# Transposed attention scores: one bank per head carried over four key tiles by key differences, and values kept by chunk

## The chip, the cores and the metric

One core of a Trainium2 chip runs the whole kernel. The metric is the device time of one execution in microseconds; before the change three runs gave a median of 2320.5 (2316.85 to 2321.68). The engines are named as in the profile: PE is TensorE's matmuls and PEld its weight loads, DVE is VectorE, ACT is ScalarE, POOL is GpSimd, SP is SyncE, which here only issues DMAs. Every engine works through its own instructions in order.

## The reference, cut to what matters

A transformer block with conditioning, for x of shape (2, 2048, 512), 16 heads of 32, hidden size 2048:

```
mod = silu(condition) @ Wada + bada            # shift, scale and gate, twice
xm  = layernorm(x) * (1 + sc_a) + sh_a
q, k, v = split(xm @ Wqkv)
attn = softmax(where(causal, q k^T / sqrt(32), -inf))
x   = x + gt_a * ((attn @ v) @ Wproj + bproj)
xm  = layernorm(x) * (1 + sc_m) + sh_m
x   = x + gt_m * (gelu(xm @ W1 + b1) @ W2 + b2)
```

## The kernel before, in words

The two batches (rows in the code) run one after the other: the QKV projection of 2048 tokens, the attention, the output projection. The MLP follows for both.

**QKV projection** (`Qkv.group`, L811). Four groups g of 512 tokens. In each, for the four chunks f of 128 channels (four heads), a tile of queries and a tile of keys is made in a PSUM bank, transposed (channels by tokens). ACT copies it in rounded form into `hl[:, 0]` (L830), DVE writes what the rounding left into `hl[:, 1]` (L831), and SP stores both to DRAM (L836). After chunk 0 the keys and queries are loaded again as `kst` and `qst` (L316, L325): for each head, the 128 partitions hold two parts of 32 channels, twice, in an order in which one matmul over 128 partitions yields the sum of all products of parts. Then come four tiles of values; ACT copies each into `vv` (L852), which holds all 2048 tokens by 512 channels of the batch. Between the projection's matmuls PE already computes scores of the first units, for their row maxima.

**Attention** (`attention_phase`, L541). A unit is a chunk c of four heads and a block i of 512 queries, 16 units per batch. For chunk 0 the blocks come in the order 0 to 3, then 0, 2, 1, 3. There are two kinds of scores. The first, tiles named `s`, have queries on partitions (`Row.bank`, L442): DVE takes their row maxima (L461, and L456 for masked ones). They are computed up to three units ahead, and `Row.score` (L494) puts them between other matmuls; the number for each step follows from `due` (L675), which spreads them over the steps by a weight for each. They use two PSUM banks. When a unit's maxima are complete, `split` (L464) divides each into three bf16 parts on DVE, and `rows` (L516) transposes them into `fold`.

The second kind, tiles named `st`, have keys on partitions (`scores_t`, L550). A step is one tile of 128 keys by 512 queries for four heads (unit i has 4i full steps, then three masked ones). Four matmuls put minus the maximum into the four heads' banks (`sel` times `fold`, 32 partitions, L575); then for each head one matmul adds the scores, and ACT writes the exponential into `e` (L593). The scores of the first kind stand between them, four or five per step as a rule: two in the two `s` banks, one in a bank borrowed from the four for `st` (L611), and again one in an `s` bank. Two steps later come the value matmuls `o` (L637). POOL adds the tiles of a group of four steps (L623), so that the row sums `sm` need one set of matmuls for four steps; in a batch's last unit DVE does this. POOL also masks (L602).

**Weights of the MLP.** During the projection POOL loads, combines and stores pieces of W1 and W2 (`Quarters`, L898), then combines W1 further (`FirstLayer`, L972), in rooms of the tag `w49`: two buffers of 7 x 512 values per partition.

Of the kernel before, what the change touches and what calls it, by code (L numbers as in the profile page):

```python
# [27 lines left out]
def dit_block_kernel(  # L28
# [69 lines left out]
    ones = bp.tile([P, P], F32, tag="ones", name="ones")  # L98
# [8 lines left out]
    nc.vector.tensor_scalar(sel, ones, -1.0, None, ALU.mult)  # L107
# [61 lines left out]
    ]  # L169
    n_early = (C - 1) * NQ  # L170
# [118 lines left out]
    class Row:  # L289


        def __init__(self, b):
            self.b = b
            self.vv = bp.tile([P, NT, D], F32, tag="vv", name="vv")
            self.kst, self.qst, self.pools = {}, {}, {0: bp}
            self.at = 0
            self.todo = [
                (u, h, t, kb)
                for u, (_, i) in enumerate(units)
                for h in range(HC)  # L300
                for t in range(TQ)
                for kb in range(i + 1)
            ]
            self.mx = None
            self.spent = 0
            self.rows_made = 0

        def load_keys(self, c, g, n=1):

            tok = slice(g * MT, (g + n) * MT)  # L310
            if g == 0:
                self.kst[c] = self.pools[c % 2].tile(
                    [P, HC, T], F32R, tag=f"kst{c % 2}", name="kst"
                )
            for r in range(4):
                nc.sync.dma_start(  # L316
                    self.kst[c][r * HD : (r + 1) * HD, :, tok].bitcast(F32),
                    kd[self.b][c][r % 2, :, tok].rearrange("(h d) t -> d h t", d=HD),
                )

# [220 lines left out]
    def attention_phase(row):  # L541
        b, vv, kst, qst = row.b, row.vv, row.kst, row.qst
        with pool(f"att{b}") as ap, pool(
# [4 lines left out]
            n_bank = [0]  # L548

            def scores_t(u, step, n):  # L550
# [21 lines left out]
                for h in range(HC):  # L572
                    g = slice(h * HD, (h + 1) * HD)
                    st = st_bank()
                    mm(  # L575
                        st[:, :w], sel[g, :], fold[u % 2][g, q0 : q0 + w],
                        start=True, stop=False,
                    )
                    sts.append(st)
                for h in range(HC):  # L580
                    at = 0
                    for j, q in tiles:
                        mm(
                            sts[h][:, at : at + QB - q],
                            kst[c][:, h, j * P : (j + 1) * P],
                            qst[u][:, h, q:],
                            start=False, stop=at + QB - q == w,
                        )
                        at += QB - q
# [94 lines left out]
            for u, (c, i) in enumerate(units):  # L684
                if NQ <= u + AHEAD < len(units):
                    row.load_queries(u + AHEAD)
                if u % NQ == 0 and c + 1 < C:
                    row.load_keys(c + 1, 0, NG)
                steps = len(steps_of[u])
                for n_step, tiles in enumerate(steps_of[u]):  # L690
                    last = n_step == steps - 1
# [37 lines left out]
                    def values(es=es, tiles=tiles, c=c, o=o, first=n_step == 0, last=last):  # L729
                        tile_by_tile(  # L730
                            o,
                            lambda j, h: vv[:, j, (c * HC + h) * HD : (c * HC + h + 1) * HD],
                            es, tiles, first, last,
                        )

                    def row_sums(es, last, tiles=((0, 0),), sm=sm, summed=summed):
                        first = not summed
                        summed.add(len(summed))
                        tile_by_tile(sm, lambda j, h: ones[:, :HD], es, tiles, first, last)
# [29 lines left out]
    class Qkv:  # L769
# [41 lines left out]
        def group(self, g, hp, between, among):  # L811
# [5 lines left out]
            n = 0  # L817
            for f in range(C):
                for which in range(2):
# [18 lines left out]
                    )  # L838
                    between(n)
                    n += 1  # L840
                if f == 0:
                    row.load_keys(0, g)
                    row.load_queries(g)
            for t in range(MTT):
# [7 lines left out]
                nc.scalar.copy(row.vv[:, g * MTT + t, :], ps)  # L852
# [41 lines left out]
    piece = 7 * C // 2 * P  # L894
# [77 lines left out]
    class FirstLayer:  # L972
# [8 lines left out]
        def load(self):  # L981
            if self.at < 7:
                room = self.pool.tile([P, 7, C * P], F32, tag="w49", name="w49", bufs=2)
                act(load_blocks(nc.gpsimd, room, 1, self.at))
# [3 lines left out]
        def step(self):  # L988
# [4 lines left out]
            n, room = self.rooms.pop(0)  # L993
            for k in range(4):
                room_sum(room, 1, k)
            act(nc.gpsimd.dma_start(w1e[n], room))
# [209 lines left out]
    with pool("qkv1") as qp, pool("ps_qkv1", bufs=6, space=PSUM) as ps_mm:  # L1206
# [18 lines left out]
        with pool("hl1") as hp:  # L1225
            late = FirstLayer(hp)

            def also(g, n):
# [3 lines left out]
                elif n % 2 == 0:  # L1232
                    late.step()

            def rooms():
                w = hp.tile([P, 7, C * P], F32, tag="w49", name="w7", bufs=2)
                w = w.rearrange("p n d -> p (n d)")
                return [w[:, k * piece : (k + 1) * piece] for k in range(2)]
# [3 lines left out]
            assert quarters.at >= FC and late.at == 7 and not late.rooms  # L1242
# [7 lines left out]
    HK = C // 2  # L1250
# [674 lines left out]
```

## Time and profile before

| | |
|---|---|
| median of three runs | 2320.5 us |
| the profiled execution | 2323.1 us |
| its span | 2321.4 us |
| granted TensorE clock | 0.998 |
| PE busy | 2270.8 us |
| DVE busy | 1582.5 us |
| POOL busy | 1290.9 us |
| first and last maximum matmul, batch 0 | 213.4 and 735 us |
| first and last maximum matmul, batch 1 | 997 and 1525 us |

Times in a row are microseconds from the span's start. A matmul's end is modelled, so matmuls that run into each other show lengths that overlap; the distance between two starts is the better price. What stands in brackets is the idle time of that engine before the instruction, and the instruction that ended it. A row "x4" is four instructions of one kind in a row.

### The profile page before, as it was taken

To read this page: it belongs to the slowest core of one execution; us is meant where nothing else is said; L and a number is where in the kernel's file an instruction comes from. 1 tells how busy PE (TensorE), PEld (TensorE's weight loads), DVE (VectorE), ACT (ScalarE), POOL (GpSimd) and SP (SyncE) were. 2 spreads that over 40 slices of the span, in tenths; PEclk is the share of its full clock that TensorE was granted. 3 is DMA by queue.
4 is the path that set the end of the run, shared out by engine and by line. 5 is a ranking of instruction groups with operands and counts; after the bars stand their busy time and mean duration, and the time that the engine had idled before them with its cause. 6 is when DMAs were issued, how large, how long until landed. Compare 5 with 4: busy or idle time off the path is not lost. (4 is left out here: it accounts for less than half of the span.)

```text
span 2321.4 us, 33398 instructions
## 1 busy us (share of the span) xinstructions
PE 2270.8 (98%) x12141; PEld 1388.8 (60%) x12141; DVE 1582.5 (68%) x3117; ACT 914.6 (39%) x1744; POOL 1290.9 (56%) x1036
## 2 busy tenths in 40 slices
PE   8999999999999999999999999999999999999998
PEld 4455545455544444555455554446888888888887
DVE  3366776777666735677667777555896876877787
ACT  2112555555565021155555554622332152251230
POOL 1052987878793663478788886653764602602510
PEclk9999999999999999999999999999999999999999
DMA  7577216151233799981522404265375554654643
GB/s 257 185 243 204 55 28 133 29 119 47 74 115 127 241 297 298 320 235 24 113 48 48 100 24 134 81 206 205 118 279 200 199 186 146 212 173 151 216 143 116
DMA packets 118524, 355.60 MB, mean 153 GB/s; under 512 B 14496, under 2 KB 15052, under 8 KB 103640
## 3 DMA queue, kind: packets, MB, share of 16 engines
q1 hardware_dynamic: 107040, 293.64, 41.9%
q0 software_dynamic: 10944, 59.28, 7.0%
q8 instruction: 96, 1.57, 0.3%
q14 instruction: 68, 0.56, 0.1%
q10 hardware_dynamic: 376, 0.55, 0.1%
HBM read 253.80 MB, written 107.48 MB: 156 GB/s over the span
## 5 line engine op out<-in xcount | busy, mean ns | idle before, releaser
L593 ACT ACTIVATE e<-st 128x512 f32<-128x512 f32 (+1 forms) x1152 | 573.1, 579 | 411.6 <-PE st L203 350.5
L461 DVE TENSOR_REDUCE mx<-s 128x1 f32<-128x512 f32 x604 | 408.0, 687 | 185.0 <-PE s L203 183.6
L623 POOL TENSOR_TENSOR ee<-ee,e 128x1024 f32<-128x1024 f32 x212 | 498.8, 2385 | 8.3 <-ACT e L593 8.3
L203 PE MATMUL s<-kst,qst 128*128 128x512 f32 (+3 forms) x1032 | 466.5, 453 | 15.9 <-DVE mx L461 6.3
L203 PE MATMUL st<-qst,kst 128*128 128x512 f32 (+3 forms) x1280 | 410.1, 387 | 0.0
L203 PE MATMUL ps_a<-sum,room 128*128 128x256 f32 x1504 | 357.4, 382 | 6.6 <-DVE c L1409 3.8
L203 PEld LDWEIGHTS ps_a<-sum,room 128*128 128x128 f32 x1504 | 281.5, 190 | 56.0 <-issue 8.7
L203 PE MATMUL o<-e,vv 128*32 128x512 f32 (+3 forms) x2560 | 300.8, 539 | 0.8 <-POOL e L602 0.8
L203 PEld LDWEIGHTS s<-kst,qst 128*128 128x128 f32 x1032 | 194.5, 189 | 174.0 <-DVE mx L461 58.6
L456 DVE CUSTOM_DVE_ANT_0 junk<-s,causal 128x512 bf16<-128x512 f32 (+3 forms) x428 | 209.2, 489 | 126.2 <-PE s L203 118.7
L203 PEld LDWEIGHTS st<-qst,kst 128*128 128x128 f32 x1280 | 227.5, 188 | 96.8 <-issue 66.7
L623 POOL TENSOR_TENSOR ee<-e 128x1024 f32<-128x1024 f32 x84 | 198.4, 2384 | 130.5 <-ACT e L593 130.4
L203 PE MATMUL ps_qk<-xmT,wqkv 128*128 128x512 f32 x512 | 240.5, 597 | 1.8 <-DVE xmT L263 1.8
L602 POOL TENSOR_SCALAR_AFFINE_SELECT e<-e 128x256 f32<-128x256 f32 x256 | 103.8, 436 | 107.2 <-ACT e L593 74.2
L203 PEld LDWEIGHTS ps_qk<-xmT,wqkv 128*128 128x128 f32 x512 | 94.2, 190 | 97.7 <-issue 91.4
L1637 POOL TENSOR_TENSOR c<-c,h 128x512 f32<-128x512 f32 x40 | 58.2, 1474 | 160.8 <-ACT c L1635 160.8
L203 PE MATMUL ps_b<-sum,room 128*128 128x256 f32 x608 | 143.6, 379 | 0.0
L203 PEld LDWEIGHTS ps_b<-sum,room 128*128 128x128 f32 x608 | 115.0, 190 | 15.4
L203 PE MATMUL ps_v<-wqkv,xmT 128*128 128x512 f32 x256 | 122.3, 594 | 0.0
L203 PEld LDWEIGHTS o<-e,vv 128*32 128x32 f32 x2560 | 60.8, 108 | 101.1 <-issue 83.4
L203 PE MATMUL st<-fold,sel 32*128 32x512 bf16 (+1 forms) x1152 | 116.1, 372 | 3.6 <-DVE mhl L482 2.6
L461 DVE TENSOR_REDUCE mx<-st 128x1 f32<-128x512 f32 x164 | 112.7, 687 | 4.9 <-PE st L203 2.7
(179 smaller groups left out, 2869.6 us busy)
## 6 DMA issues: line engine op xcount, KB each, us to landing
qst<-q SPq DMA_DIRECT2D x128, 256.0 KB
room<-w1e SPq DMA_DIRECT2D x28, 1024.0 KB
kst<-k SPq DMA_DIRECT2D x24, 1024.0 KB
room<-w1e SPq DMA_DIRECT2D x28, 768.0 KB
room<-w2e SPq DMA_DIRECT2D x21, 1024.0 KB
q<-hl SPq DMA_DIRECT2D x32, 512.0 KB
k<-hl SPq DMA_DIRECT2D x32, 512.0 KB
room<-w2e SPq DMA_DIRECT2D x21, 768.0 KB
```

The source lines that it names most:

```text
L203: return tc.keep_in_program_order(nc.tensor.matmul(*args, **kw))
L456: nc.vector.tensor_tensor_reduce(junk[:, :w], s[:, :w], causal[:, QB - w :], 1.0, MASKED, ALU.add, ALU.max, m,)
L461: nc.vector.tensor_reduce(m, s[:, :w], axis=AX.X, op=ALU.max)
L593: act(nc.scalar.activation(e[:, h % 2, :w], sts[h][:, :w], AF.Exp))
L602: nc.gpsimd.affine_select(d, d, pattern=[[0, 2], [1, P]], compare_op=ALU.is_ge, fill=0.0, base=0, channel_multiplier=-1,)
L623: act(engine.tensor_tensor(dst, x, y, ALU.add))
L1637: nc.gpsimd.tensor_tensor(c, c, piece_of(base, i, t, pair), ALU.add)
```

## The change

In the full steps of a unit the four heads' banks are kept for a group of four key tiles. The first tile of a group is computed as before: minus the maximum, plus the scores. For each of the next three, a matmul with the difference between this key tile and the one before it is added to the bank, which then holds the scores of this tile minus the maximum. Masked steps are as before. Where the next step adds to the kept banks, the scores of the first kind no longer borrow one of them.

The differences are made in the projection, for the first three token groups: ACT copies the key tile, DVE subtracts it from its neighbour, ACT and DVE write the two parts into `dl` (one buffer), and SP stores them after the next tile's store. They are loaded as `dst`, one tile for each of three token groups, for chunk 0 in the projection and for later chunks in steps 6, 10 and 14 of the last unit of a chunk.

The values no longer stay on chip for the whole batch: chunk 0 is copied into a tile of one chunk, the other three go through DRAM (`vt`, `vd`) and are loaded one chunk ahead, in two buffers. `FirstLayer` works on halves, in three buffers of half the size, and is called on each tile of the projection instead of every second. `ones` is narrower, and `sel` is made from the identity.

```diff
@@ class Row
+        def load_differences(self, c, g):
+            t = bp.tile([P, HC, MT - P], F32R, tag=f"dst{g}", name="dst")
+            for r in range(4):
+                nc.sync.dma_start(
+                    t[r * HD : (r + 1) * HD].bitcast(F32),
+                    dd[self.b][c][r % 2, :, g].rearrange("(h d) t -> d h t", d=HD),
+                )
+            self.dst[c, g] = t
+        def new_values(self, c):
+            self.vv[c] = bp.tile([P, NT, P], F32, tag="vv", name="vv", bufs=2)
+        def load_values(self, c):
+            self.new_values(c)
+            nc.sync.dma_start(self.vv[c], vd[self.b][:, :, c * P : (c + 1) * P])
@@ attention_phase
+            def by_difference(u, step):
+                return step % TQ > 0 and step < units[u][1] * TQ
...
-                for h in range(HC):
-                    g = slice(h * HD, (h + 1) * HD)
-                    st = st_bank()
-                    mm(
-                        st[:, :w], sel[g, :], fold[u % 2][g, q0 : q0 + w],
-                        start=True, stop=False,
-                    )
-                    sts.append(st)
+                differ = by_difference(u, step)
+                if differ:
+                    sts = banks[0]
+                else:
+                    for h in range(HC):
+                        g = slice(h * HD, (h + 1) * HD)
+                        st = st_bank()
+                        mm(
+                            st[:, :w], sel[g, :], fold[u % 2][g, q0 : q0 + w],
+                            start=True, stop=False,
+                        )
+                        sts.append(st)
+                    banks[0] = sts
...
+                        if differ:
+                            keys = row.dst[c, j // TQ][:, h]
+                            keys = keys[:, (j % TQ - 1) * P : j % TQ * P]
+                        else:
+                            keys = kst[c][:, h, j * P : (j + 1) * P]
...
-                    row.score(1, st_bank)
+                    row.score(1, None if by_difference(u, step + 1) else st_bank)
...
-                    weight.append(1250 + (12 if n < i * TQ else 14) * w // 2)
+                    fixed = 800 if by_difference(u, n) else 1250
+                    weight.append(fixed + (12 if n < i * TQ else 14) * w // 2)
...
+                if u % NQ == 2 and c + 1 < C:
+                    row.load_values(c + 1)
...
+                    if u % NQ == NQ - 1 and c + 1 < C and n_step in (6, 10, 14):
+                        row.load_differences(c + 1, n_step // TQ - 1)
@@ Qkv.group
+                    for store in late:
+                        store()
+                    late.clear()
+                    if which and g < NG - 1:
+                        before = hp.tile([P, MT - P], F32, tag="before", name="before", bufs=2)
+                        act(nc.scalar.copy(before, ps[:, : MT - P]))
+                        d = ps[:, P:]
+                        act(nc.vector.tensor_tensor(d, d, before, ALU.subtract))
+                        dl = hp.tile([P, 2, MT - P], F32R, tag="dl", name="dl", bufs=1)
+                        act(nc.scalar.activation(dl[:, 0, :], d, AF.Copy))
+                        act(
+                            nc.vector.tensor_tensor(
+                                dl[:, 1, :], d, dl[:, 0, :].bitcast(F32), ALU.subtract
+                            )
+                        )
+                        late.append(
+                            lambda dl=dl, f=f: nc.sync.dma_start(
+                                dd[b][f][:, :, g].rearrange("l p t -> p l t"),
+                                dl.bitcast(F32),
+                            )
+                        )
...
-                nc.scalar.copy(row.vv[:, g * MTT + t, :], ps)
+                if not row.vv:
+                    row.new_values(0)
+                nc.scalar.copy(row.vv[0][:, g * MTT + t, :], ps[:, :P])
+                vt = hp.tile([P, D - P], F32, tag="vt", name="vt", bufs=2)
+                nc.scalar.copy(vt, ps[:, P:])
+                nc.sync.dma_start(vd[b][:, g * MTT + t, P:], vt)
@@ FirstLayer.load, FirstLayer.step
-                room = self.pool.tile([P, 7, C * P], F32, tag="w49", name="w49", bufs=2)
-                act(load_blocks(nc.gpsimd, room, 1, self.at))
+                room = self.pool.tile([P, 7, HK * P], F32, tag="w49", name="w49", bufs=3)
+                n, half = self.at // 2, slice(self.at % 2 * HK, (self.at % 2 + 1) * HK)
...
-            act(nc.gpsimd.dma_start(w1e[n], room))
+            w = HK * P
+            act(nc.gpsimd.dma_start(w1e[at // 2][:, :, at % 2 * w : (at % 2 + 1) * w], room))
```

More of the change, by code (lines that the diff above doesn't have):

```diff
@@ L106, in dit_block_kernel @@
     nc.vector.tensor_copy(ident_h, ident)
-    nc.vector.tensor_scalar(sel, ones, -1.0, None, ALU.mult)
+    nc.vector.tensor_scalar(sel, ident, 0.0, -1.0, ALU.mult, ALU.add)
     tmask = bp.tile([P, TQ + 1], F32, tag="tmask", name="tmask")
@@ L169, in dit_block_kernel @@
     ]
+    dd = [
+        [
+            dram.tile([2, P, NG - 1, MT - P], F32, tag=f"d{b}{c}", name=f"d{b}{c}")
+            for c in range(C)
+        ]
+        for b in range(B)
+    ]
+    vd = [dram.tile([P, NT, D], F32, tag=f"v{b}", name=f"v{b}") for b in range(B)]
     n_early = (C - 1) * NQ
@@ L1231, in also @@
                         quarters.step()
[L1232 removed]
+                else:
                     late.step()
             def rooms():
[L1236 to L1238 removed]
+                w = hp.tile([P, 7, HK * P], F32, tag="w49", name="w7", bufs=3)
+                return [w.rearrange("p n d -> p (n d)")]
             quarters.more_rooms = rooms
             qkv.run(hp, also)
[L1242 removed]
+            assert quarters.at >= FC and late.at == 14 and not late.rooms
     attention_phase(row)
@@ L1249, in dit_block_kernel @@
     HF = FC // 2
-    HK = C // 2
     with ExitStack() as mlp:
```

35 lines of the change are left out of this document (23 added, 12 removed).

## The prediction

> **What bounds the kernel now.** I read the page's busy times first, then the stages, then one step of attention instruction by instruction, and last the waits in the QKV projection. One core's execution:
>
> ```profile
> span 2321.4 us, 33398 instructions
> PE 2270.8 (98%) x12141; PEld 1388.8 (60%) x12141; DVE 1582.5 (68%) x3117; ACT 914.6 (39%) x1744; POOL 1290.9 (56%) x1036
> ```
>
> Busy times of two stretches, the middle of each batch's attention; columns are length, then PE, PEld, DVE, ACT, POOL, granted clock, DMA share, GB/s:
>
> ```profile
> 250.00:690.00 440.00, 435.11 (x3043) 221.52 (x3040) 308.06 (x779) 247.81 (x495) 361.99 (x242) 1.00 0.29 73
> 1032.00:1480.00 448.00, 438.57 (x3048) 222.25 (x3040) 313.37 (x786) 247.62 (x494) 363.53 (x241) 1.00 0.29 73
> ```
>
> PE has 5 to 9 us of idle in 440; POOL has 82% and DVE 70%. So work taken from PE is worth its full time here, unless PE then waits for another engine. DMA is three tenths used and no limit in this stage.
>
> One step of attention (from the timeline of three engines): start, length, instruction, idle before it.
>
> ```profile
> 307.48 0.39 PE L203 MATMUL st<-fold,sel 32*128 32x512 bf16 x4
> 307.81 0.50 PE L203 MATMUL st<-qst,kst 128*128 128x512 f32 x1
> 308.15 0.39 PE L203 MATMUL s<-kst,qst 128*128 128x512 f32 x1
> 308.40 2.06 ACT L593 ACTIVATE e<-st 128x512 f32<-128x512 f32 x4 [1.50 <-PE st L203]
> 308.57 0.69 DVE L461 TENSOR_REDUCE mx<-s 128x1 f32<-128x512 f32 x1 [0.29 <-PE s L203]
> 308.60 0.34 PE L203 MATMUL s<-kst,qst 128*128 128x384 f32 x1
> 309.18 0.55 DVE L456 CUSTOM_DVE_ANT_0 junk<-s,causal 128x384 bf16<-128x384 f32 x1
> 309.25 0.40 PE L203 MATMUL st<-kst,qst 128*128 128x512 f32 x1
> 309.48 0.39 PE L203 MATMUL s<-kst,qst 128*128 128x512 f32 x1
> 309.68 0.69 DVE L461 TENSOR_REDUCE mx<-st 128x1 f32<-128x512 f32 x1
> 309.80 1.07 PE L203 MATMUL o<-e,vv 128*32 128x512 f32 x8
> 310.80 0.40 PE L203 MATMUL st<-fold,sel 32*128 32x512 bf16 x4
> ```
>
> The step takes 3.32 us from maximum matmul to maximum matmul (310.80 - 307.48). It holds four transposed score tiles (st), and four score tiles of later units (s), whose row maxima VectorE takes. The third of these (309.25) is in a borrowed st bank, so the fourth (309.48) returns to the first s bank, whose reduction, begun at 308.57, was done at 309.26. Hence nobody waits.
>
> **What the change takes from PE.** Full tiles come in groups of four, and in the last three the maximum isn't added again. Each batch has 4 x (4 + 8 + 12) = 96 full steps; three quarters, over two batches, is 144 steps. In each the next matmul starts 0.33 us after the maximum matmuls (307.81 - 307.48): 144 x 0.33 = 47.5 us. The other bound is the group of all such matmuls: 106.4 us over 256 sets of four, 0.416 each, 60 us; it counts ends that overlap the next matmul, so I take 47.5.
>
> ```profile
> L203 PE MATMUL st<-fold,sel 32*128 32x512 bf16 x1024 | 106.4, 384 | 3.3 <-DVE mhl L482 2.6 <-ACT vv L852 0.4
> ```
>
> The score matmuls with key differences have the shape of those they replace: nothing. Their bank must be emptied by ACT's exponential of the step before. Four of those take 2.06 us and begin 0.59 us after a step's first score (308.40 - 307.81), so the first bank is free some two microseconds before the next step: nothing.
>
> **What it costs in the same steps.** Where the next step continues the sums, all four st banks must stay, and the borrow is dropped (the None handed to the score call). In the order of the changed build's instructions, 126 steps, namely the first three of each four outside the last unit, have four of these scores ahead of the value matmuls and only two banks for them. Then the fourth waits for the second's reduction, not the first's. How such a wait looks now:
>
> ```profile
> 643.34 0.63 DVE L456 CUSTOM_DVE_ANT_0 junk<-s,causal 128x512 bf16<-128x512 f32 x1
> 643.89 0.08 DVE L456 DVE_READ_ACCUMULATOR2_ANT mx<- 128x1 f32 x1
> 644.03 0.19 PEld L203 LDWEIGHTS s<-kst,qst 128*128 128x128 f32 x1 [0.27 <-DVE mx L456]
> 644.04 0.48 PE L203 MATMUL s<-kst,qst 128*128 128x512 f32 x1
> 644.45 1.06 PE L203 MATMUL o<-e,vv 128*32 128x512 f32 x8
> 650.11 1.29 DVE L461 TENSOR_REDUCE mx<-s 128x1 f32<-128x512 f32 x2 [0.55 <-PE s L203]
> 300.10 0.82 DVE L526 TENSOR_TENSOR fold<-ps_m,tmask 128x640 bf16<-128x640 bf16 x1 [1.90 <-PE ps_m L522]
> ```
>
> The weight load is held too: it starts 0.06 after VectorE is done (643.97 to 644.03), and the value matmuls follow 0.41 after that matmul's start instead of 0.32 (309.80 - 309.48). Counted from a step's first score: the first reduction begins at 0.76 (308.57 - 307.81), and two full ones take 1.29, so the second is done at 2.05; then 0.06 + 0.42 puts the value matmuls at 2.53, against 1.99 now (309.80 - 307.81). That is 0.54 us. A masked tile of 384 reduces 0.1 faster (0.50 from 309.18 to 309.68, against 0.60 for each of a pair), and one of 128 about 0.4 faster; over the four widths I take 0.19 less, 0.35. By the order, the first two scores are both full in 58 steps, mixed in 66, both narrow in 2: 58 x 0.54 + 66 x 0.35 + 2 x 0.15 = 55 us. Low bound 0.30 a step (the second reduction overlaps more), 38 us; high bound 0.60 (76 us), because VectorE also writes the next maxima (0.82 us, once per unit) and splits them, which a third bank partly absorbed. For these I add 5 us.
>
> Attention: -47.5 + 55 + 5 = +12 us, between -22 (60 saved, 38 lost) and +33 (48, 76, 5). Within it, the last units (18 of the 144 steps, without foreign scores) gain 6 us, and steps that keep the maximum but lose the borrow lose about 0.45 each. The planner's lower weight for such steps moves scores, and makes none fewer. POOL's sums, ready at 82%, aren't asked to go faster.
>
> **What it costs in the projection.** For each of 24 (chunk, token group) pairs: two ACT passes and two VectorE passes over 128x384, about 0.5 us each (ACT: between 0.38 for 256 columns, below, and 0.52, a quarter of the 2.06 above; VectorE by the 0.55 at 309.18), and 32 more ACT copies. ACT is busy 2 to 7 of 20 us in the two windows below, and hides its part. VectorE's part, 24 x 1.1 = 26 us, lies beside projection matmuls, and it has a third of its time free there; its danger is order, not time. There is one buffer for the differences (dl), its store is handed to SP behind the next query store, and ACT, then VectorE, stand before it until it has landed. Behind them in VectorE's queue are the maxima for which PE's next scores need banks. How long a store takes here, and what a held VectorE does to PE:
>
> ```profile
> L593 ACT ACTIVATE e<-st 128x256 f32<-128x256 f32 x128 | 42.2, 383 | 46.2 <-PE st L203 43.7 <-POOL ee L623 1.7
> 902.50 0.39 SPq L836 DMA_DIRECT2D k<-hl  x1
> 914.36 1.20 SPq L316 DMA_DIRECT2D kst<-k  x2
> 917.50 0.43 SPq L836 DMA_DIRECT2D q<-hl  x1
> 912.04 0.68 DVE L831 SCALAR_TENSOR_TENSOR hl<-ps_qk,hl 128x512 fp32r<-128x512 f32 x1
> 899.36 2.22 DVE L244 TENSOR_SCALAR x<-x,mv,rstd 128x512 f32<-128x512 f32 x4
> 902.83 0.50 PE L203 MATMUL s<-kst,qst 128*128 128x512 f32 x1 [3.17 <-DVE mx L461]
> 904.15 1.75 PE L203 MATMUL ps_qk<-xmT,wqkv 128*128 128x512 f32 x2
> 909.05 1.02 PE L203 MATMUL ps_qk<-xmT,wqkv 128*128 128x512 f32 x2
> 900.00:920.00 20.00, 17.17 (x46) 8.87 (x47) 13.25 (x33) 2.15 (x4) 7.96 (x8) 0.91 0.90 276
> ```
>
> SP, in order, stood from 902.9 to 914.4 until a key store had landed. The new difference store of that chunk comes behind the query store of 917.5, so at 918, and lands some 6 us later by my estimate (about half the 11.4 here, on a queue that is no longer blocked), while the next chunk's keys are through VectorE at 912.7 and want the buffer at once: up to 10 us one time, 2 to 3 in other places. For group 2 of the second batch I take 6, for its other pairs 3; for the first batch, where DMA is less full, 4. Bounds: 0 (PE's six projection banks cover it) and 25.
>
> The trace also shows a gate: after 3.17 us of idle a pair of projection matmuls took 1.75 instead of 1.02, and the clock granted in that window was 0.91. The Trainium skill, "TensorE: Matmul & The Clock Gate", section "HAM oscillation", gives about 3.4 us of idle as what lets the clock fall to half; the trace agrees within its window. By it each long stall would cost some 3 us more, which is the excess of the rows from 904.15 on; it is inside the upper bound.
>
> DMA grows by 41 MB (24 difference stores of 393 KB; 32 value stores and 96 difference loads of 197 KB; 6 value loads of 1 MB) over today's 356, and 10 MB of it (12 of these difference stores, 16 value stores, 12 loads) fall into the second batch's projection. There the engines are full, and POOL's combining of W1 is paced by its stores:
>
> ```profile
> DMA packets 118524, 355.60 MB, mean 153 GB/s; under 512 B 14496, under 2 KB 15052, under 8 KB 103640
> 937.41 0.58 POOL L996 DMA_DIRECT2D w1e<-w  x1 [0.30 <-POOL w L963]
> 944.89 0.53 POOL L968 DMA_DIRECT2D w<-w1d  x1 [6.91 <-DMA w1e<-w]
> 1000.54 0.58 POOL L996 DMA_DIRECT2D w1e<-w  x1 [0.30 <-POOL w L963]
> 1001.13 2.28 POOL L602 TENSOR_SCALAR_AFFINE_SELECT e<-e 128x256 f32<-128x256 f32 x6
> 980.00:1000.00 20.00, 19.82 (x65) 9.83 (x63) 14.41 (x34) 6.98 (x12) 10.87 (x10) 1.00 1.03 400
> ```
>
> POOL is free at 1001.1, when attention wants its masks. 10 MB at 276 to 400 GB/s is 25 to 37 us of DMA. Against that, half rooms in three buffers let POOL sum one half while another's store lands, and today it idles about 7 us in each of seven rounds. I take +3 us, bounds 0 and 25. Smaller edits (the narrower ones, sel) cost nothing: they are set up once. The value loads of the later chunks fall in attention with DMA at 0.29.
>
> **Sum.** +12 in attention, +13 for the difference stores (6 + 3 + 4), +3 for POOL: +28. The profiled execution took 2323.1, 2.6 above the median of 2320.5; 2320.5 + 28 is 2348.
>
> **Rivals.**
> *The saving shows* (0.24). The price of the missing bank is under 0.38 us a step (47.5 / 126), because VectorE's reduction of the second score ends earlier against PE than I laid out, and six PSUM banks cover the difference stores. At the low bounds, -22 and nothing else: 2299. For it: PE waits for VectorE very little in attention now. Against: those few waits come with three banks.
> *DMA decides* (0.18). The difference stores hold VectorE for their upper bound (25 in place of 13) and POOL reaches attention late by its own (25 in place of 3): 2320.5 + 12 + 25 + 25 = 2382. The point is a store that lands later than one projection tile after its issue. For it: a DMA share of 0.9 to 1.0 and POOL just in time. Against: the first batch's projection is emptier, and the new rooms overlap.
> *Nothing measurable* (0.08): wait and saving cancel, and the projection covers its part: 2318 to 2325.
>
> **How the numbers follow.** My forecast has 0.50: 2348, its own range 2326 to 2372. Below it lies the first rival, above it the second; 2298 to 2384 leaves out about two in ten. A change under 0.2% (5 us) can't be told from none. Faster 0.24, same 0.08, slower 0.68.
>
> **What would show it.** Maximum matmuls: 576 instead of 1152. In the timeline a middle step of four should take 3.2 to 3.5 us, its first 3.6 to 3.8, its last 3.0. TensorE's weight-load waits for VectorE's maxima should grow by some 40 to 60 us. In the projection ACT's difference copies should wait for DMA, with PE waits for maxima beside them. I am wrong if full-width steps without the third bank run under 3.2 us, or PE's wait for maxima hardly grows.

## The result and the profile after

The changed kernel took 2405.4 us, the median of four runs (2401.1 to 2413.3), beside 2319.4 for the kernel before (four runs too). The ratio is 1.0375, with a 95% interval of 1.0345 to 1.0404: slower by 80 to 94 us. The forecast was 2348 in a range that ended at 2384. Its sign was right, its size was a third.

The first lines of the page after, one core's execution:

```profile
span 2403.0 us, 32585 instructions
PE 2278.5 (95%) x11565; PEld 1377.7 (57%) x11565; DVE 1607.7 (67%) x3165; ACT 942.5 (39%) x1824; POOL 1314.1 (55%) x1078
```

PE issues 576 matmuls fewer and is busy 8 us longer, and of the 82 us that the span grew 74 are time in which PE stands idle. The stages tell where. Busy times of five stretches, before and then after: projection of the first batch, attention, output projection with the second batch's projection, attention, MLP. Columns are length, then PE, PEld, DVE, ACT, POOL, granted clock, DMA share, GB/s.

```profile
0.00:214.00 214.00, 203.41 (x611) 100.06 (x612) 110.47 (x282) 42.70 (x75) 46.80 (x74) 1.00 0.69 224
214.00:742.00 528.00, 520.91 (x3663) 261.46 (x3663) 367.29 (x868) 302.80 (x607) 403.86 (x281) 1.00 0.32 81
742.00:997.00 255.00, 249.36 (x681) 120.18 (x678) 141.72 (x307) 40.97 (x73) 133.41 (x157) 0.99 0.88 292
997.00:1533.00 536.00, 524.55 (x3666) 262.55 (x3667) 372.16 (x875) 303.63 (x608) 408.42 (x285) 1.00 0.33 85
1533.00:2321.00 788.00, 772.59 (x3528) 644.57 (x3528) 590.89 (x787) 224.47 (x383) 298.46 (x243) 1.00 0.54 184
```

```profile
0.00:242.00 242.00, 212.23 (x614) 102.75 (x614) 125.30 (x307) 54.77 (x115) 47.32 (x74) 0.96 0.75 238
242.00:779.00 537.00, 516.93 (x3376) 253.41 (x3373) 368.05 (x866) 304.26 (x608) 406.12 (x281) 1.00 0.40 99
779.00:1073.00 294.00, 256.98 (x676) 123.10 (x676) 155.54 (x335) 53.38 (x113) 157.19 (x201) 0.95 0.88 295
1073.00:1619.00 546.00, 520.89 (x3373) 254.69 (x3373) 374.06 (x870) 304.91 (x608) 405.95 (x280) 0.99 0.39 97
1619.00:2403.00 784.00, 771.48 (x3533) 643.76 (x3529) 584.80 (x787) 225.16 (x383) 297.48 (x244) 1.00 0.55 186
```

Attention is longer by 9 and 10 us, the MLP shorter by 4, and the two projections are longer by 28 and 39. So 67 of 82 us are lost where the new operands are made, and 15 net where they are used.

In the two projections PE stood still seven times for over 4 us, apart from the wait ahead of its first matmul (7.6 us, and 7.0 before); before, its longest stop there was the 3.17 us shown in the prediction. The seven, 42.4 us together, from the timeline of PE:

```profile
93.47 2.12 PE L219 MATMUL ps_xt<-ident,x 128*128 128x128 f32 x8 [4.42 <-DVE x L252]
156.51 0.45 PE L219 MATMUL ps_xt<-ident,x 128*128 128x128 f32 x1 [6.45 <-DVE x L252]
241.74 0.39 PE L211 MATMUL st<-fold,sel 32*128 32x512 bf16 x3 [4.27 <-ACT vt L923]
913.53 0.45 PE L219 MATMUL ps_xt<-ident,x 128*128 128x128 f32 x1 [10.53 <-DVE x L252]
960.22 0.58 PE L211 MATMUL s<-kst,qst 128*128 128x256 f32 x1 [4.70 <-DVE mx L482]
985.11 2.12 PE L219 MATMUL ps_xt<-ident,x 128*128 128x128 f32 x8 [7.92 <-ACT hl L874]
1073.33 0.61 PE L211 MATMUL st<-fold,sel 32*128 32x512 bf16 x2 [4.08 <-ACT vt L923]
```

Four of the seven, 29 us, stand before `ps_xt`, the transposes of the next token group's normalised tokens x. They don't all end with the same wait. The timeline of SP, ACT and DVE ahead of the longest (rows between those shown are left out) tells what x waited for there, with two rows of before for comparison:

```profile
882.06 5.39 SPq L333 DMA_DIRECT2D dst<-d  x4
...
896.78 0.48 ACT L923 COPY vt<-ps_v 128x384 f32<-128x384 f32 x1 [0.41 <-DMA v<-vt]
897.28 0.33 SPq L924 DMA_DIRECT2D v<-vt  x1
897.71 1.23 SPq L825 DMA_DIRECT2D x<-in_x_dram  x1
899.25 1.02 SPq L924 DMA_DIRECT2D v<-vt  x1
900.36 3.02 SPq L825 DMA_DIRECT2D x<-in_x_dram  x3
907.57 0.69 DVE L223 BATCH_NORM_STATS2 stat<-x 128x6 f32<-128x512 f32 x1 [3.23 <-DMA x<-in_x_dram]
```

```profile
842.34 3.18 SPq L781 DMA_DIRECT2D x<-in_x_dram  x4
885.74 4.25 SPq L781 DMA_DIRECT2D x<-in_x_dram  x4
```

SP works in order. The loads of x stand behind the third and fourth value store; those wait for ACT's copies into `vt`; and these wait, with two buffers, until an earlier value store has landed, which itself went out behind four loads of differences that held SP for 5.39 us. Counted from the first matmul of the output projection (742.4 before, 779.1 after), group 2's tokens are asked for at 119 to 121 instead of 100 us, group 3's at 192 (the first at 971.4) instead of 143. In the first batch it is 82.4 instead of 67.0 and 142.6 instead of 114.6. Part of that is delay that had already piled up. In the longest stop the chain of waits runs through x's landing, statistics and normalisation on VectorE to PE's transposes; its longest piece there (start, length, what):

```profile
902.08 8.32 DMA x<-in_x_dram
```

The stop at 985.11 ends otherwise: ACT could write its next `hl`, and free PE's bank, only when an earlier key store had landed, and that store had stood on SP behind three loads of x. The chain's piece:

```profile
976.08 8.35 DMA k<-hl
```

x itself was normalised from 984.18 on. In both stops the two paths end within a microsecond of each other: in the longest, too, a key store that had stood behind loads of x let ACT go on at 912.65. In the first batch neither is what ended last. VectorE took the statistics of x there without a wait, right behind an `hl` (of 88.32 in the first stop, 151.17 in the second). The first stop's:

```profile
88.92 0.68 DVE L223 BATCH_NORM_STATS2 stat<-x 128x6 f32<-128x512 f32 x1
```

That is 4.6 us ahead of the transposes (93.47); before, the statistics began 14.3 us ahead of them (70.88 and 85.22), and PE did not wait. So those two stops, 10.9 us, end with VectorE's order. Whether this order follows from the late tokens isn't shown: in the run with more buffers, below, x is asked for at 120.14, the statistics start at 136.79, and PE still stops for 4.83 us before the transposes at 143.09. Of the other three stops, two end with ACT's copy into `vt`, which had waited for an earlier value store (3.75 and 3.56 us), and the one at 960.22 with VectorE's maxima, behind two landings of `dl`.

Attention's own change is in the waits. Columns: who waited for whom, us in total, times, longest. Before, then after (L487 and L482 after are L461 and L456 before):

```profile
PEld s L203 <- DVE mx L461: 58.6, 84, 3.6
PEld s L203 <- DVE mx L456: 37.0, 52, 2.4
```

```profile
PEld s L211 <- DVE mx L487: 116.8, 244, 3.5
PEld s L211 <- DVE mx L482: 58.5, 110, 5.5
ACT dl L892 <- DMA d<-dl: 33.9, 9, 8.3
DVE dl L894 <- ACT dl L892: 29.9, 10, 7.3
ACT vt L923 <- DMA v<-vt: 20.3, 9, 3.9
```

PE's weight loads wait 80 us more for the row maxima (175.3 against 95.6). ACT's waits for the difference and value stores are the new ones. POOL's wait for its own stores fell from 42.2 to 11.3 us.

### The profile page after: what moved, and what is told of

It reads as the page before. It is cut to its first block, busy times and chain, and to the rows that moved or that the text cites. A ratio compares the mean times of both kernels' runs of the same rounds, so it can differ in the third digit from the quotient of the medians.

```text
span 2403.0 us, 32585 instructions
## 1 busy us (share of the span) xinstructions
PE 2278.5 (95%) x11565; PEld 1377.7 (57%) x11565; DVE 1607.7 (67%) x3165; ACT 942.5 (39%) x1824; POOL 1314.1 (55%) x1078
## 4 chain that ended last, share of the span: by engine, by line
PE 79%; DVE 13%; DMA 4%; issue 2%; POOL 1%; ACT 1%; SPq 0%; DVEq 0%; POOLq 0%; ACTq 0%
PE ps_a L211 14%; PE st L211 12%; PE s L211 10%; PE o L211 10%; PE ps_qk L211 8%; PE ps_b L211 7%; DVE mx L487 5%; PE ps_o L211 4%; PE ps_v L211 4%; PE sm L211 4%; PE ps_c L211 3%; DVE junk L482 1%; PE ps_xt L219 1%; DVE sum L1368 1%; DMA d<-dl 1%
## 5 line engine op out<-in xcount | busy, mean ns | idle before, releaser
L632 ACT ACTIVATE e<-st 128x512 f32<-128x512 f32 (+1 forms) x1152 | 578.3, 578 | 415.1 <-PE st L211 354.5
L487 DVE TENSOR_REDUCE mx<-s 128x1 f32<-128x512 f32 x696 | 467.0, 688 | 242.6 <-PE s L211 237.5
L211 PE MATMUL s<-kst,qst 128*128 128x512 f32 (+3 forms) x1156 | 533.0, 466 | 47.0 <-DVE mx L487 17.6
L211 PEld LDWEIGHTS s<-kst,qst 128*128 128x128 f32 x1156 | 219.8, 190 | 263.6 <-DVE mx L487 116.8
L482 DVE CUSTOM_DVE_ANT_0 junk<-s,causal 128x128 bf16<-128x128 f32 (+3 forms) x460 | 223.8, 487 | 118.3 <-PE s L211 109.9
L211 PE MATMUL ps_qk<-xmT,wqkv 128*128 128x512 f32 x512 | 247.8, 612 | 3.4 <-DVE xmT L271 1.8
L211 PE MATMUL st<-qst,dst 128*128 128x512 f32 x576 | 207.9, 416 | 0.0
L211 PE MATMUL st<-qst,kst 128*128 128x512 f32 (+2 forms) x704 | 201.2, 361 | 0.0
L211 PEld LDWEIGHTS st<-qst,dst 128*128 128x128 f32 x576 | 105.5, 189 | 83.8 <-ACT e L632 60.5
L211 PEld LDWEIGHTS st<-qst,kst 128*128 128x128 f32 x704 | 122.3, 190 | 47.3 <-issue 32.4
L1016 POOL DMA_DIRECT2D w<-in_L_cond_W_dram x64 | 41.2, 659 | 147.4 <-DMA dst<-d 121.4
```

What stands on the lines that cost most here:

```text
L211: return tc.keep_in_program_order(nc.tensor.matmul(*args, **kw))
L482: nc.vector.tensor_tensor_reduce(junk[:, :w], s[:, :w], causal[:, QB - w :], 1.0, MASKED, ALU.add, ALU.max, m,)
L487: nc.vector.tensor_reduce(m, s[:, :w], axis=AX.X, op=ALU.max)
L632: act(nc.scalar.activation(e[:, h % 2, :w], sts[h][:, :w], AF.Exp))
L1016: nc.gpsimd.dma_start(w[:, n], src)
```

## Experiments

Two theories. **Mine, after the result:** attention costs what was forecast (a bank instead of a matmul), and the rest is the projection, where stores that wait for their producers stand in SP's queue and in front of single buffers. **The rival:** attention costs more than the stages show, or the projection's loss is plain work and bytes (passes, 41 MB more DMA), the same in any order.

### Attention alone

The changed attention in the kernel before, with its projection untouched:

```diff
+                differ = by_difference(u, step)
+                if differ:
+                    sts = banks[0]
+                else:
...
                         mm(
                             sts[h][:, at : at + QB - q],
                             kst[c][:, h, j * P : (j + 1) * P],
...
+                    row.score(1, None if by_difference(u, step + 1) else st_bank)
...
+                    fixed = 800 if by_difference(u, n) else 1250
```

> The kernel before with the change's attention alone: the maximum is added once per four tiles and no bank is borrowed ahead of a tile that continues the sums; the three other tiles multiply with the keys themselves instead of key differences, which are neither made, stored nor loaded, and the values stay whole (so the scores computed are other ones). If attention pays back what it saves and the projection makes the rest of the loss: about +16 us, 2336, with the projection stages as before (first maximum matmul near 213 us). If the loads of differences and values disturb attention itself: clearly below 2320, since the saving of 47 us would show.

Measured: 2336.2, ratio 1.0053 (1.0037 to 1.0069), +12 us. The forecast for attention was +12. How it comes about is seen in the next run, the kernel before in which only the borrowing is dropped:

```diff
-                    row.score(1, st_bank)
+                    row.score(1, None if by_difference(u, step + 1) else st_bank)
```

> The kernel before with the borrowed bank alone taken away, in the same 126 steps; all maxima are still added. If the second reduction is what the value matmuls wait for: a group of four full steps grows by 1.2 us (0.40 in three of its steps), +45 to +55 us in all, 2370. If the two banks were enough and attention's small loss comes from scores that the planner moved to masked steps: within 10 us of 2320.

Measured: 2371.6, ratio 1.0207 (1.0190 to 1.0224), +48 us for 126 steps, 0.38 each. The row of PE's weight loads for these scores (count, busy, mean; idle before them and its causes), before and in this run:

```profile
L203 PEld LDWEIGHTS s<-kst,qst 128*128 128x128 f32 x1032 | 194.5, 189 | 174.0 <-DVE mx L461 58.6 <-issue 44.7 <-DVE mx L456 37.0
```

```profile
L203 PEld LDWEIGHTS s<-kst,qst 128*128 128x128 f32 x1158 | 217.8, 188 | 248.4 <-DVE mx L461 127.4 <-DVE mx L456 52.8 <-issue 42.5
```

The count rises by just the 126 scores that no longer borrow, and the wait for maxima by 85 us. So the maxima saved, less what the scores cost that the planner moves, give back 36 of the 48.

Can the saving be had by putting the scores elsewhere? Two tries, both on top of attention alone. In the first, the fourth score goes behind the value matmuls:

```diff
+                    if by_difference(u, step + 1):
+                        return es, n - 3
                     row.score(1, None if by_difference(u, step + 1) else st_bank)
```

> As e1_attention_only, with the fourth score of a step without the borrowed bank put behind the value matmuls instead of ahead of them. If the wait for the second reduction is the price: it disappears and the saving shows, 2320 - 47 + about 10 for scores moved, 2275 to 2290. If the price lies elsewhere: 2330 to 2340 as in e1.

Measured: 2344.0, ratio 1.0082 (1.0065 to 1.0099). Neither range held it: the wait didn't go, it moved to the next scores, and grew (in attention alone this row has 112.3).

```profile
PEld s L203 <- DVE mx L461: 158.8, 293, 2.6
```

In the second, such steps take at most three scores:

```diff
+                    if by_difference(u, n_step + 1):
+                        n = min(n, 3)
```

> As e1_attention_only, with at most three scores in a step that can't borrow; the planner gives the rest to the other steps. If the fourth score's wait for the second reduction is the price, full steps lose it, and the steps that take more scores pay part of it back: 2290 to 2320. If what bounds a step is VectorE's chain of reductions over two banks wherever the scores stand (as e3_attention_fourth_later suggests): 2330 or more.

Measured: 2346.9, ratio 1.0119 (1.0099 to 1.0139). From the maximum matmuls of one group of four steps to the next (42 groups outside the last units) the mean is 15.30 us before, 15.51 in the changed kernel, and 14.80 here: 21 us are saved in the full steps. But the scores have to go somewhere: the masked steps become 54 us longer than before (in order of the three masked tiles: before 3.68, 4.11, 3.05 us; in the changed kernel 3.87, 4.28, 3.18, without the two stops of 4.27 and 4.08 that fall into the first; here 4.60, 4.76, 3.27). So a wait between PE and VectorE for the banks came up wherever the scores were put. What the moved scores cost by themselves isn't settled: in this run the granted clock also fell to 0.50 for 6.8 us in six places of attention, which can be up to 20 us of the 54 (half of PE's 39 us of busy time there).

### The projection alone

The changed kernel with attention as before (`by_difference` is always false):

```diff
-                return step % TQ > 0 and step < units[u][1] * TQ
+                return False
```

> The changed kernel with the attention of before: every tile adds its maximum and borrows its bank; differences are made, stored and loaded (and not read), values go through DRAM by chunk, W1 is combined in halves. If the projection stages hold the loss: +60 to +70 us, 2385, with attention as long as before (about 529 us from the first maximum matmul to the first output projection matmul). If attention's loads cost something: attention longer than 535 too.

Measured: 2389.4, ratio 1.0276 (1.0259 to 1.0294), +64 us. So the projection is nearly the whole loss. Taken apart from the bottom up, with every edit below made to this kernel, first without differences at all:

```diff
-                    if which and g < NG - 1:
+                    if False:
...
-                    row.load_differences(0, g)
```

> As e4_projection_only, with the differences neither made nor stored nor loaded; what is left of the change is values by chunk through DRAM and W1 in halves. If the one difference buffer and its stores make the projection's loss: about 2330, at most +15. If the value stores, each of which SP takes in order while later loads of x and of keys stand behind it, make it: 2360 or more.

Measured: 2327.5, ratio 1.0026 (1.0014 to 1.0038), +6 us. Values by chunk, their stores and loads, and W1 in halves cost only this.

Then the differences made, but neither stored nor loaded:

```diff
-                        late.append(lambda dl=dl, f=f: nc.sync.dma_start(...))
...
-                    row.load_differences(0, g)
```

> The differences are made (two ACT and two VectorE passes for each of the 24 pairs) but neither stored nor loaded; values by chunk and the W1 halves as changed, attention as before. The passes alone, with no store to wait for. Theory A, the passes hide beside the projection's matmuls: as without differences, 2326 to 2331. Theory B, the two VectorE passes and the longer hold of a PSUM bank cost PE time directly: 1.1 us for each of 24 pairs, 26 us on top, 2345 to 2355.

Measured: 2329.1, ratio 1.0034 (1.0023 to 1.0045), +8 us. The four passes for each of 24 tiles cost about 2 us (+-4), not clear of nothing: work beside PE is hidden, as forecast. Then made and stored:

```diff
-                        row.load_differences(c + 1, n_step // TQ - 1)
-                    row.load_differences(0, g)
```

> The projection's part of the change with attention as before, the differences made and stored but never loaded (the 96 loads are left out; nothing reads the differences there). With the loads it cost 67 us; without them and with three buffers for the differences and four for the values it cost 20. Theory A, the single buffer is what costs (ACT stands until a store has landed): taking away the loads alone leaves most of it, 2375 to 2389. Theory B, the loads on SP cost (the first chunk's loads stand on SP until the last difference store has landed, and the token loads stand behind them): as with more buffers, 2338 to 2350. I hold A.

Measured: 2362.3, ratio 1.0175 (1.0155 to 1.0196), +41 us. Neither range held it: 24 stores from one buffer cost 33 us (+-5), and the loads on top another 23 (+-6). (Such bounds, here and below, are the roots of the summed squares of the two intervals' half widths.) In this run SP asks for all four x tiles together (873.90, 114 us after the output projection's first matmul at 759.9), and PE waits little for them; what is left is the chain that the prediction had named, a store that ACT and then VectorE wait for. Two waits of this run:

```profile
ACT dl L890 <- DMA d<-dl: 37.2, 11, 8.2
```

```profile
PE ps_xt L219 <- DVE x L252: 7.3, 4, 4.4
```

The second in the projection alone, with the loads:

```profile
PE ps_xt L219 <- DVE x L252: 39.0, 8, 15.3
```

The same without loads, and with more buffers, three for the differences and four for the values:

```diff
-                        dl = hp.tile([P, 2, MT - P], F32R, tag="dl", name="dl", bufs=1)
+                        dl = hp.tile([P, 2, MT - P], F32R, tag="dl", name="dl", bufs=3)
-                vt = hp.tile([P, D - P], F32, tag="vt", name="vt", bufs=2)
+                vt = hp.tile([P, D - P], F32, tag="vt", name="vt", bufs=4)
```

> As e4_projection_only without the loads of differences (nobody reads them there), which makes room for three difference buffers instead of one and four value buffers instead of two; all stores stay on SP. If ACT's and VectorE's wait for the one buffer is the cause: the loss falls from 66 to under 25 us. If SP's order is: the stores still wait there for ACT and DVE with x and the keys behind them, and 35 us or more stay.

Measured: 2341.8, ratio 1.0093 (1.0077 to 1.0109), +22 us, so the buffers, of differences and values together, are worth 19 (+-6). ACT's wait for difference stores is gone from the list of waits.

Now the queue. In the projection alone, with one buffer and with loads, the stores are issued by ACT, so that they don't stand in front of SP's loads:

```diff
-                            lambda dl=dl, f=f: nc.sync.dma_start(
+                            lambda dl=dl, f=f: nc.scalar.dma_start(
-                nc.sync.dma_start(vd[b][:, g * MTT + t, P:], vt)
+                nc.scalar.dma_start(vd[b][:, g * MTT + t, P:], vt)
```

> As e4_projection_only, with the stores of differences and values issued by ACT, right after the instructions that fill their buffers, instead of SP. If SP's order is the cause (a store that isn't ready holds the loads of x, keys and queries behind it, and lets its own buffer come free late): the loss falls from 66 to under 25 us. If DMA bandwidth in the projection is the cause, the same bytes move and the loss stays at 50 us or more.

Measured: 2359.8, ratio 1.0161 (1.0134 to 1.0188): 27 us (+-7) better than by SP, with nothing computed or moved less. That part of the loss is order, neither work nor bytes. The Trainium skill, "Perfetto Trace Analysis", section "DMA Optimizations", says that it may make sense to issue inputs from one engine and outputs from another, above all around loops and control flow. Here only the stores of differences and values were moved, and these 27 us agree. The run doesn't part loads that are no longer held behind stores from buffers that come free earlier: ACT's wait for difference stores fell too, from 30.0 to 20.1 us.

What remains is 37 us, between the two ranges. It contains a stop of 13.87 us for PE when the second attention starts. From the timeline of POOL and PE, with rows between left out:

```profile
1036.97 2.87 POOL L1039 TENSOR_TENSOR w<-w 128x256 f32<-128x256 f32 x4 [9.62 <-DMA w<-w1d]
1040.93 2.36 POOL L641 TENSOR_SCALAR_AFFINE_SELECT e<-e 128x256 f32<-128x256 f32 x6
1041.58 2.27 PE L211 MATMUL o<-e,vv 128*32 128x512 f32 x8 [13.87 <-POOL e L641]
```

PE's value matmuls waited for POOL's masks, and these stood on POOL behind the last piece of W1, whose data POOL had waited for. (The chain of waits names a load of keys that landed at 1040.95, but the mask had begun at 1040.93.) The exponentials to be masked were all there by 1028.06. So this is the late POOL of the rival "DMA decides", and it shows once PE gets through the projection sooner.

With both, more buffers and ACT's queue, and no loads:

> No difference loads, three buffers for the differences and four for the values, and the difference and value stores are issued by ACT instead of SP. With SP this cost 20 us. Theory A: what is left is SP's order (token loads behind stores that wait for ACT's copies): 2326 to 2332, near the 6 us that the value part alone cost. Theory B: what is left is the work of the passes and the DMA bytes, the same on either queue: 2338 to 2345.

Measured: 2336.2, ratio 1.0073 (1.0052 to 1.0094), +17 us. Against SP's queue with the same buffers this is 5 us (+-6), which is no difference: with the buffers there, the queue made no difference that these runs can tell. Nor is it as good as without stores (+8); the 9 us between (+-6) are nearer to the second theory's range. Whether they are bytes or the stores' place in time these runs don't tell.

### The whole change with ACT's queue

> The whole change, with the difference and value stores issued by ACT instead of SP. In the projection alone this took the loss from 67 to 38. If the parts add up: the changed kernel's 2405 less 29, 2370 to 2382. If ACT's issue costs attention or the wait has another cause there: 2390 or more.

Measured: 2368.4, ratio 1.0203 (1.0183 to 1.0223), +47 us: better than the changed kernel by 40 us (+-8), and 10 us (+-8) above the projection alone with that queue, where attention alone makes 12. The parts add up here, within the noise. In the kernel as changed the parts leave something: 64 and 12 make 76, against 87 (80 to 94) measured; the profiled executions (spans of 2390.9 for the projection alone and 2403.0) are 12 apart, as the parts would have it. More than that isn't settled. POOL is late in the run with ACT's queue too: PE stops for 11.36 us at 1046.38, again before value matmuls and behind POOL's masks.

No run beat the kernel before, and the parts say why: even with a projection that cost nothing, the changed attention is 12 us slower. A third bank for the first kind of scores was not tried.

## Why the prediction was right and wrong

**Attention: the total right, in part by luck.** Its +12 was measured as +12 (9 to 16) alone; in the changed kernel the two attention stretches are 9 and 10 us longer, and the MLP, which the diff doesn't touch, 4 shorter. The wait came where it was laid out. One group of four after, PE's matmuls at the start of each step, and the value matmuls:

```profile
403.69 0.40 PE L211 MATMUL st<-fold,sel 32*128 32x512 bf16 x4
404.02 0.50 PE L211 MATMUL st<-qst,kst 128*128 128x512 f32 x1
406.44 1.06 PE L211 MATMUL o<-e,vv 128*32 128x512 f32 x8
407.78 0.39 PE L211 MATMUL st<-qst,dst 128*128 128x512 f32 x1
410.44 1.07 PE L211 MATMUL o<-e,vv 128*32 128x512 f32 x8
411.43 0.50 PE L211 MATMUL st<-qst,dst 128*128 128x512 f32 x1
413.97 1.06 PE L211 MATMUL o<-e,vv 128*32 128x512 f32 x8
...
418.76 0.39 PE L211 MATMUL st<-fold,sel 32*128 32x512 bf16 x4
```

From a step's first score to its value matmuls it is 2.42, 2.66 and 2.54 us in the three steps without the third bank; 2.53 was laid out, 1.99 was the value before. The sum's terms, though, were off, and cancelled. The missing bank cost 48 us when alone, where 55 + 5 was taken and 38 was the low bound. The saving was well sized: from the run without the borrow to attention alone, groups shrink from 16.51 to 15.57 us (42 of them, 39.5 us) and the last units by 6.7, together 46 where 47.5 was taken. But between the same two runs the masked steps grew by 12 us, and nothing in the sum stood for them: "the planner's lower weight moves scores, and makes none fewer" overlooked where they go. So the +12 came of a bank priced 12 too high and of 12 us that were left out. In the changed kernel the masked steps are 14.5 us longer than before; with 9 us more in the groups and 8 less in the last units (6 were forecast) this makes about 16 of the 19 that the two stretches show.

Three details were off. The lengths forecast for single steps (3.2 to 3.5 in the middle) were too short, since they were counted from one quick step of 3.32 us, while the mean step is 15.30 / 4 = 3.83. Counted from first score to first score, the steps of a group changed by +0.17, +0.09, +0.01 and -0.09 us; the middle ones are near the forecast, the first (+0.3 to +0.5) and the last (-0.3) are not. And PE's weight loads waited 80 us more for maxima, 69 more with attention alone, where 40 to 60 were forecast.

**Projection: the sign right, the size wrong.** The term "+13 for the difference stores (6 + 3 + 4), bounds 0 and 25" is what failed, and with it the loads of differences, which stood in the sum as MB only. In the projection alone it is 64 less 6 less 2 = 56 us: 33 for the stores, 23 for the loads.

The mechanism I named for the stores is there, ACT and VectorE held by the one buffer's store (33.9 and 29.9 us of waits after). It was sized by the longest single landing and a guess of "2 to 3 in other places"; nine such waits were measured, up to 8.3 us each. Three of them, 10.6 us, are in the first batch, where I took 4 because "DMA is less full"; that projection lost 28 us.

What I did not follow is SP's queue past the stores. I costed 32 value stores as "32 more ACT copies" and as bytes, 96 loads as bytes, and never asked what stands on SP behind a load that takes long to issue or a store that waits for its copy. There stood the next group's tokens, asked for 15 to 49 us later than before, and behind them key stores that ACT waits for. Two of the seven stops, 18 us, end with these. The two before the first batch's transposes end with VectorE's order, and that this comes of the late tokens is not shown.

**"DMA decides" was nearer in time than my forecast, for half of its reason.** It set 25 for the stores and 25 for a late POOL. POOL was not late:

```profile
1043.03 0.95 POOL L1079 DMA_DIRECT2D w1e<-w  x1 [0.30 <-DVE mx L482]
1076.24 0.40 POOL L641 TENSOR_SCALAR_AFFINE_SELECT e<-e 128x256 f32<-128x256 f32 x1 [32.26 <-ACT e L632]
```

It was done 32 us before attention needed it. My +3 was nothing here, but because PE was slow, not because POOL was quick: counted from the output projection's first matmul, POOL's last store of W1 is issued after 264 us (1043.03 - 779.1), before after 258 (1000.54 - 742.4). Where the projection was hardly longer, in the run without differences, the masks stood right behind that store (1006.47 and 1005.68), as before; with ACT's queue POOL was late, by the stops of 13.87 and 11.36 us above. The bytes were right (356 to 396 MB, 41 forecast). What they cost as bytes isn't settled: with three buffers and ACT's queue the stores leave 9 us (+-6), and no run tells the bytes of the loads from what they hold up on SP.

**The clock: right in kind, too small in count.** Each long stop is followed by matmuls at half speed. One stretch right behind a stop (columns as above; the clock is the third figure from the end):

```profile
93.40:97.00 3.60, 3.53 (x11) 2.41 (x11) 3.29 (x7) 1.61 (x3) 0.00 (x0) 0.50 0.96 224
```

In the projections PE's busy time grew by 8.8 and 7.6 us (212.23 - 203.41 and 256.98 - 249.36) for nearly the same count of matmuls, 2.3 for each of the seven stops. I put this "inside the upper bound" for one stop, at some 3 us; the rows named for that hold about 1.6 (starts of 904.15, 906.12 and 907.95, where later pairs come every 1.09), and there were seven stops. The Trainium skill, "TensorE: Matmul & The Clock Gate", section "HAM oscillation", puts the limit at about 3.4 us of idle. All seven stops were longer, and the clock agrees: 0.50 in the 3.5 us behind six of them, 0.59 behind the one of 4.27 us. The kernel before falls a little short of that figure: its stop of 3.17 us was followed by 0.58 and 0.57 (904 to 906 and 906 to 908), while one of 2.63 us in the changed kernel, before 1028.58, was followed by 1.00.

**"The saving shows"** fell: the price of the missing bank was to be under 0.38 us a step and was 0.38 (0.35 to 0.41), which alone would not decide; attention alone is 9 to 16 us slower, and the cover by six banks that it counted on did not hide the stores' 33 us.

## What to carry to other kernels

When a change adds a store to an in-order queue, write down what stands behind it there and ask when its data will be ready: a store that waits for its copy, which waits for a buffer, which waits for an earlier store, delays every load behind it. Here the queue alone gave 27 us back, and more buffers 19 of the stores' 33, while the passes that made the data cost 2. No run changed both and kept the loads. When a slow stage gets quicker, look at what it had been hiding: here POOL's work on W1. And a matmul saved on the bounding engine is worth its time only if the same step keeps the banks that the others use to hand over: 0.33 us were saved and 0.38 paid in a step.

## What the runs showed of the hardware that I had not expected

Four loads of 192 KB each held SP's queue for 2.90 us in the first batch (issued at 71.60) and for 5.39 at 882.06, and everything behind them on the queue paid. The DMA share was 1.0 in both stretches, so what makes the second slower stays open. And the granted clock fell without any long stop: in the run with three scores per step it was 0.50 for 6.8 us in six places of attention (415.1, 558.5, 701.9, 1210.5, 1353.8 and 1500.6), and PE had no stop over 0.55 us in the 7 us ahead of any of them.
